# Moving the last quarter of a set-up weight product into the first graph's chain of products

## The chip, the cores and the metric

One core of one Trainium2 chip runs the whole program. The metric is the device time of one execution, in microseconds (us).

## The reference, cut to what matters

There are 64 graphs of 256 nodes and 512 features. Each passes a graph layer with a residual and a norm, then an attention layer with the same frame:

```python
def L0(x, adj, W):                                 # layer 0
    deg = jnp.sum(adj, axis=-1, keepdims=True)
    agg = jnp.einsum('bij,bjf->bif', adj, x) / jnp.maximum(deg, EPS)
    return jax.nn.relu(jnp.einsum('bnf,of->bno', jnp.concatenate([x, agg], axis=2), W))
def L1(X, adj, mask, Wqk, Wv):                     # layer 1
    q, k = jnp.split(X @ Wqk, 2, axis=-1)
    v = X @ Wv
    agg = jnp.einsum('bij,bjd->bid', adj, k * mask[:, :, None])
    w = inv_scale * mask * jnp.einsum('bid,bid->bi', q, agg)
    return jax.nn.softmax(w, axis=1)[:, :, None] * v
x = _layernorm(x + L0(x, adj, L0_gnn_W))
x = _layernorm(x + L1(x, adj, nodemask, L1_gnn_Wqk, L1_gnn_Wv))
```

The kernel never forms q and k. It multiplies the two halves of `Wqk` once, at the start. This "product of weights" is a 512x512x512 float32 product, and its result `w1[:, :4]` is used by layer 1 alone. Layer 1 of the first graph begins at about 66 to 69 us, long after its layer 0.

## The kernel before

The set-up product: 16 matmul instructions, which the profile shows as 32 records (two for each float32 instruction), all ahead of the first graph.

```python
ps = [ps_mm.tile([P, F], F32, name="mm") for _ in range(NF)]
for a in range(NA):                                # NA = NF = 4
    for c in range(NF):
        nc.tensor.matmul(ps[c], wqk[:, a, c * P:(c + 1) * P], wqk[:, NA + a, :], start=(a == 0), stop=(a == NA - 1))
for c in range(NF):
    nc.scalar.copy(w1[:, c, :], ps[c])
```

Every other product is done by a scheme with seven products instead of eight. It needs sums of the weights (on VectorE, once for each layer) and of the rows (for each graph, on GpSimd for layer 0 and on VectorE for layer 1). The four sums of a layer are called T1 to T4 here:

```python
def weight_sums(w, name):                          # W0 for layer 0, W1 for layer 1
    ...
    nc.vector.tensor_sub(t1, b12, b11)             # T1
    nc.vector.tensor_sub(t2, b22, t1)              # T2
    nc.vector.tensor_sub(b12, b22, b12)            # T3
    nc.vector.tensor_sub(t4, b21, t2)              # T4
```

Layer 0 of a graph is five products, then two. The sixth waits until `u` has been copied out, and the gather with `adj` waits for the last addition. The first graph has nothing else to run in these two waits. Later graphs run layer 1 of an earlier graph there.

```python
def layer0_a(g):
    ...                                            # u = A11.B11; p5 = S1.T1; u += S2.T2; p2 = A12.B21
    product(u, s["S3"], w["T3"], start=False)
    nc.scalar.copy(y[:, 1, :], u)                  # the sixth product waits for this
    nc.vector.tensor_add(y[:, 1, :], p5, y[:, 1, :])
def layer0_b(g):
    product(u, s["A22"], w["T4"], start=False)     # sixth
    nc.scalar.copy(own[:, 1, :], u)
    product(p5, s["S4"], w["B22"], start=False)    # seventh
    nc.vector.tensor_add(y[:, 0, :], p5, y[:, 0, :])   # the gather waits for this
```

The gather makes four sums `tv` on VectorE, seven half-width products on TensorE and additions into `zr`. The norm's chain follows: `combine0` and `layer_norm` on VectorE, masked copies on ScalarE, then a transpose.

The loop over graphs, cut:

```python
W0 = weight_sums(w0, "t0_")
for i in range(B + LAG - 1):
    if i == 1:
        W1 = weight_sums(w1, "t1_")
    ...
    layer0_a(i)
    ...
    layer0_b(i)
    ...                                            # gather, combine0, norm0
```

The order of instructions on an engine is not the order of these lines: a scheduler sets it. `tc.issue_after(x)` holds the instructions of its block behind `x` in that order.

Of the kernel before, what the change touches and what calls it, by code (L numbers as in the profile page):

```python
# [35 lines left out]
F32 = mybir.dt.float32  # L36
# [4 lines left out]
P = 128  # L41
Q = 32
LAG = 4
DEG_EPS = 1e-6
LN_EPS = 1e-5
# [3 lines left out]
def resnorm_kernel(  # L49
# [12 lines left out]
    nc = tc.nc  # L62
    B, N, F = x.shape
    A = wqk_t.shape[0] // 2
    NT, NF, NA = N // P, F // P, A // P
    H, HF = NF // 2, F // 2
# [4 lines left out]
    const = ctx.enter_context(tc.tile_pool(name="const", bufs=1))  # L71
    pool = ctx.enter_context(tc.tile_pool(name="pool", bufs=2))
    small = ctx.enter_context(tc.tile_pool(name="small", bufs=4))
    ps_mm = ctx.enter_context(tc.tile_pool(name="ps_mm", bufs=8, space=bass.MemoryType.PSUM))
# [5 lines left out]
    def first(out, in_):  # L80

        return tc.keep_in_program_order(nc.sync.dma_start(out, in_))

    def load(g, dma=nc.sync.dma_start):
        adjs[g] = pool.tile([P, NT, N], F32, name="adj", bufs=4)
        dma(adjs[g], adj_t[g].rearrange("(t p) i -> p t i", p=P))
        rows[g] = pool.tile([P, NT, N], F32, name="rows")
        dma(rows[g], adj[g].rearrange("(t p) j -> p t j", p=P))
        xs[g] = pool.tile([P, NT, F], F32, name="x", bufs=3)
        dma(xs[g], x[g].rearrange("(t p) f -> p t f", p=P))  # L90
        return load_t(g, dma)

    def load_t(g, dma):
        if g not in xTs:
            xTs[g] = pool.tile([P, NF, N], F32, name="xT")
            return dma(xTs[g], x_t[g].rearrange("(c p) n -> p c n", p=P))


    w0 = const.tile([P, 2 * NF, F], F32, name="w0")
    w1 = const.tile([P, 2 * NF, F], F32, name="w1")  # L100
    setup = tc.tile_pool(name="setup", bufs=1)
    with setup as sp:
        wqk = sp.tile([P, 2 * NA, F], F32, name="wqk")
        for a in range(NA):
            src = wqk_t.rearrange("(h a p) f -> a p h f", p=P, h=2)[a]
            first(wqk.rearrange("p (h a) f -> a p h f", h=2)[a], src)
        w0_of = w_t.rearrange("(k h p) o -> k p h o", p=P, h=H)
        for k in (0, 2):
            first(w0[:, k * H:(k + 1) * H, :], w0_of[k])
        load_t(0, first)  # L110
        for k in (3, 1):
            first(w0[:, k * H:(k + 1) * H, :], w0_of[k])
        load(0, first)
        mask_sb = const.tile([P, NT, B], F32, name="mask_sb")
        first(mask_sb, mask_t)
        load_t(1, first)
        load(1, first)
        loaded = first(w1[:, NF:, :], wv.rearrange("(c p) o -> p c o", p=P))

        ident = const.tile([P, P], F32, name="ident")  # L120
        make_identity(nc, ident)
        eps = const.tile([P, 1], F32, name="eps")
        nc.vector.memset(eps, LN_EPS)
        wide = [const.tile([P, Q], F32, name=f"wide{k}") for k in (0, 1)]
        for w in wide:
            nc.vector.memset(w, 0.0)

        ps = [ps_mm.tile([P, F], F32, name="mm") for _ in range(NF)]
        for a in range(NA):
            for c in range(NF):  # L130
                nc.tensor.matmul(ps[c], wqk[:, a, c * P:(c + 1) * P], wqk[:, NA + a, :],  # L131
                                 start=(a == 0), stop=(a == NA - 1))
        for c in range(NF):
            nc.scalar.copy(w1[:, c, :], ps[c])
    late = ctx.enter_context(tc.tile_pool(name="late", bufs=2))

    def weight_sums(w, name):
        b11, b21, b12, b22 = (w[:, k * H:(k + 1) * H, :] for k in range(4))
        t1, t2, t4 = (const.tile([P, H, F], F32, name=f"{name}{k}") for k in (1, 2, 4))
        nc.vector.tensor_sub(t1, b12, b11)  # L140
        nc.vector.tensor_sub(t2, b22, t1)  # L141
        nc.vector.tensor_sub(b12, b22, b12)
        nc.vector.tensor_sub(t4, b21, t2)
        return {"B11": b11, "B21": b21, "B22": b22, "T1": t1, "T2": t2, "T3": b12, "T4": t4}
# [13 lines left out]
    def product(ps, a, b, start=True):  # L158
        for c in range(H):
            nc.tensor.matmul(ps, a[:, c, :], b[:, c, :], start=start and c == 0, stop=(c == H - 1),  # L160
                             skip_group_check=True)

    def bank():
        return ps_mm.tile([P, F], F32, name="mm")
# [26 lines left out]
    def prepare(g):  # L191
        deg = small.tile([P, NT], F32, name="deg")
        r = rows.pop(g)
        for t in range(NT):
            nc.scalar.activation(r[:, t, :], r[:, t, :], AF.Copy, accum_out=deg[:, t:t + 1])
        rdegs[g] = small.tile([P, NT], F32, name="rdeg")
        nc.vector.tensor_scalar(rdegs[g], deg, DEG_EPS, None, op0=OP.max)
        nc.vector.reciprocal(rdegs[g], rdegs[g])
        a, sa = adjs[g], pool.tile([P, 4, P], F32, name="sa", bufs=3)
        a11, a21, a12, a22 = a[:, 0, :P], a[:, 0, P:], a[:, 1, :P], a[:, 1, P:]  # L200
        nc.gpsimd.tensor_add(sa[:, 0], a21, a22)  # L201
        nc.gpsimd.tensor_sub(sa[:, 1], sa[:, 0], a11)
        nc.gpsimd.tensor_sub(sa[:, 2], a11, a21)
        nc.gpsimd.tensor_sub(sa[:, 3], a12, sa[:, 1])
        sumsA[g] = {"A11": a11, "A12": a12, "A22": a22, "S1": sa[:, 0], "S2": sa[:, 1], "S3": sa[:, 2],
                    "S4": sa[:, 3]}
        sums0[g] = row_sums(xTs.pop(g), nc.gpsimd)

    def layer0_a(g):
        s, w = sums0[g], W0  # L210
        own = owns[g] = pool.tile([P, NT, F], F32, name="own")
        y = values(g)[:, 0]
        u, p5, p2 = bank(), bank(), bank()
        product(u, s["A11"], w["B11"])
        began = nc.scalar.copy(own[:, 0, :], u)  # L215
        product(p5, s["S1"], w["T1"])
        product(u, s["S2"], w["T2"], start=False)
        nc.scalar.copy(y[:, 0, :], u)
        product(p2, s["A12"], w["B21"])
        added = nc.vector.tensor_add(own[:, 0, :], p2, own[:, 0, :])  # L220
        product(u, s["S3"], w["T3"], start=False)
        nc.scalar.copy(y[:, 1, :], u)  # L222
        nc.vector.tensor_add(y[:, 1, :], p5, y[:, 1, :])
        open0[g] = u, p5
        return began, added

    def layer0_b(g):
        s, w, own, y = sums0.pop(g), W0, owns[g], values(g)[:, 0]
        u, p5 = open0.pop(g)
        product(u, s["A22"], w["T4"], start=False)  # L230
        nc.scalar.copy(own[:, 1, :], u)
        product(p5, s["S4"], w["B22"], start=False)
        nc.vector.tensor_add(y[:, 0, :], p5, y[:, 0, :])  # L233

    def values(g):

        if g not in vals:
            vals[g] = pool.tile([P, 2, NT, F], F32, name="vals")
        return vals[g]
# [68 lines left out]
    def layer1_steps(g):  # L308
        sc, part = scores[g] = (small.tile([P, NT], F32, name="scores", bufs=3),
                                small.tile([P, 1], F32, name="part", bufs=3))  # L310
        s, w, agg = sums1.pop(g), W1, aggs.pop(g + 1)[:, 1]
        v = vs[g] = late.tile([P, NT, F], F32, name="v", bufs=LAG)
# [87 lines left out]

    W0 = weight_sums(w0, "t0_")
    prepare(0)
    def step(gen, n=1):
        for _ in range(n):
            next(gen, None)

    for i in range(B + LAG - 1):
        new = i < B
        if i + 2 < B:
            with tc.issue_after(loaded.ins):  # L410
                loaded = load(i + 2)
        if i == 1:
            W1 = weight_sums(w1, "t1_")
        if 0 <= i - 3 < B - 2:
            write_scores(i - 3)
            read_scores(i - 3)
        if new:
            began, added = layer0_a(i)
        if 0 <= i - 2 < B:
            turn(i - 2)  # L420
        l1 = layer1_steps(i - 2) if 0 <= i - 2 < B else iter(())
        step(l1)
        if new:
            layer0_b(i)
        if i - 3 >= B - 2:
            softmax_turned(i - 3)
            finish(i - 3)
        if i <= B:
            z, summed = gather_a(i)
        step(l1, 2)  # L430
        step(z)
        if 0 <= i - LAG < B - 2:
            with tc.issue_after(began.ins), tc.issue_after(added.ins):
                softmax(i - LAG)
            with tc.issue_after(summed.ins):
                finish(i - LAG)
        for _ in range(4):
            step(l1)
            step(z)
        if new:  # L440
            combine0(i)
            norm0(i)
        if i + 1 < B:
            with tc.issue_after(began.ins), tc.issue_after(added.ins):
                prepare(i + 1)
# [26 lines left out]
```

## Time and profile before

| kernel before | |
|---|---|
| time, median of 3 runs | 1988.32 us (1986.9 to 1988.72) |
| profiled span | 1986.5 us |
| set-up product: first matmul to the first layer-0 product | 15.60 us (4.67 to 20.27) |
| first layer-0 product (A) to first product of the fourth graph (M) | 70.64 us (20.27 to 90.91): **S** |
| M to the first layer-1 product of the last graph but one | 1848.0 us (90.91 to 1938.92) |
| from there to the end | 47.6 us |

The row marked S begins after TensorE's wait for the first load and after its warm-up, and it ends when TensorE has been without a gap for some 20 us. The prediction shows TensorE's side of the start. This is VectorE's timeline of the same stretch (start in us, length, engine, line, operation, output<-inputs, shape, count, and in brackets the idle time before with its releaser):

```profile
29.68 0.69 DVE L223 TENSOR_TENSOR vals<-mm,vals 128x512 f32<-128x512 f32 x1 [1.03 <-ACT vals L222]
30.28 1.22 DVE L140 TENSOR_TENSOR t<-w 128x1024 f32<-128x1024 f32 x1
...
32.68 1.22 DVE L142 TENSOR_TENSOR w<-w 128x1024 f32<-128x1024 f32 x1
33.81 0.68 DVE L233 TENSOR_TENSOR vals<-mm,vals 128x512 f32<-128x512 f32 x1
...
41.53 0.75 DVE L291 SCALAR_TENSOR_TENSOR own<-zr,rdeg,own 128x512 f32<-128x512 f32 x1 [0.81 <-ACT zr L281]
...
46.05 0.66 DVE L220 TENSOR_TENSOR own<-mm,own 128x512 f32<-128x512 f32 x1
46.74 1.00 DVE L188 TENSOR_SCALAR x<-own,mv,rstd 128x512 f32<-128x512 f32 x2
```

Three of layer 1's sums (from 30.28 us) stand ahead of the addition of line 233, for which the gather waits. The chain of the first norm begins at 41.53 and has its result `x` from 46.74 on, 5.21 us later.

### The profile page before, as it was taken

Reading aid. Unit: us, or ns where it says so; the run is one execution under the profiler, and the core shown is the slowest. Engines: PE = TensorE matmul, PEld = TensorE weight load, DVE = VectorE, ACT = ScalarE, POOL = GpSimd, SP = SyncE. Lnnn points to the kernel's source line nnn. Section 1 sums busy time; section 2 is a strip of 40 time slices with the busy share of each in tenths; the row PEclk is TensorE's granted clock in tenths of the full one; section 3 lists DMA queues with packets and bytes.
Section 4 is the critical chain, followed back from the end, with each engine's and each line's share of the span. In section 5 each row is a group of like instructions: output and inputs, shape, how many; then the busy total and the mean of one; then the engine's idle time right before and its main releaser. Section 6 shows DMA issues by size and latency. Waiting matters only on the chain.

```text
span 1986.5 us, 19676 instructions
## 1 busy us (share of the span) xinstructions
PE 1960.3 (99%) x5416; PEld 1017.5 (51%) x5416; DVE 1566.5 (79%) x3218; ACT 650.0 (33%) x1543; POOL 419.6 (21%) x518
## 2 busy tenths in 40 slices
PE   8999999999999999999999999999999999999996
PEld 3554555555555545555555555555555555555552
DVE  5677877888788788778878887887787788878877
ACT  2323333333233333333332333333333333323332
POOL 3122221221221221222212212212222122122100
PEclk9999999999999999999999999999999999999999
DMA  6333333333333333333333333333333333333221
GB/s 223 88 83 82 98 94 85 95 91 90 96 80 100 93 83 103 93 81 95 91 90 95 83 98 94 83 102 93 81 95 92 89 96 81 101 96 80 80 45 56
DMA packets 394830, 182.62 MB, mean 92 GB/s; under 512 B 285793, under 2 KB 359393, under 8 KB 394721
## 3 DMA queue, kind: packets, MB, share of 16 engines
q1 hardware_dynamic: 394720, 181.36, 34.0%
q8 instruction: 44, 0.72, 0.2%
q14 instruction: 66, 0.53, 0.1%
HBM read 114.10 MB, written 33.62 MB: 74 GB/s over the span
## 4 chain that ended last, share of the span: by engine, by line
PE 96%; DVE 1%; SPq 1%; DMA 0%; ACT 0%; issue 0%; DVEq 0%
PE mm L160 76%; PE mm L259 19%; SPq L175 1%; PE mm L131 1%; DVE st L182 0%; DMA adj<-adj_t 0%; DMA wqk<-wqk_t 0%; DVE own L293 0%; DVE own L291 0%; DMA x1T<-sq 0%; DVE x L188 0%; DVE o L396 0%; ACT vals L300 0%; DVE v L341 0%; DVE t L141 0%
## 5 line engine op out<-in xcount | busy, mean ns | idle before, releaser
L160 PE MATMUL mm<-w,s 128*128 128x512 f32 x1024 | 481.5, 592 | 0.8 <-ACT v L327 0.8
L160 PE MATMUL mm<-t,s 128*128 128x512 f32 x1024 | 461.4, 593 | 0.2 <-ACT q L320 0.2
L160 PEld LDWEIGHTS mm<-t,s 128*128 128x128 f32 x1024 | 194.7, 190 | 243.7 <-issue 228.2
L160 PEld LDWEIGHTS mm<-w,s 128*128 128x128 f32 x1024 | 194.2, 190 | 192.8 <-issue 155.0
L160 PE MATMUL mm<-w,x1T 128*128 128x512 f32 x512 | 241.4, 594 | 3.9 <-DMA x1T<-sq 3.9
L160 PE MATMUL mm<-w,xT 128*128 128x512 f32 x512 | 240.9, 592 | 0.0
L201 POOL TENSOR_TENSOR sa<-adj 128x128 f32<-128x128 f32 x64 | 45.8, 716 | 760.2 <-PE mm L259 758.7
L152 POOL TENSOR_TENSOR s<-xT 128x256 f32<-128x256 f32 x64 | 46.8, 731 | 706.3 <-PE mm L160 687.3
L259 PE MATMUL mm<-tv,sa 128*128 128x256 f32 x768 | 187.4, 379 | 0.6 <-DVE tv L249 0.4
L259 PEld LDWEIGHTS mm<-tv,sa 128*128 128x128 f32 x768 | 145.7, 190 | 76.3 <-issue 48.2
L233 DVE TENSOR_TENSOR vals<-mm,vals 128x512 f32<-128x512 f32 x64 | 44.2, 691 | 142.9 <-PE mm L160 142.9
L185 ACT ACTIVATE rstd<-mv,eps 128x2 f32<-128x2 f32 x128 | 37.9, 296 | 341.3 <-DVE mv L183 341.3
L160 PEld LDWEIGHTS mm<-w,x1T 128*128 128x128 f32 x512 | 97.2, 190 | 98.9 <-issue 95.6
L160 PEld LDWEIGHTS mm<-w,xT 128*128 128x128 f32 x512 | 97.3, 190 | 94.7 <-issue 91.4
L327 ACT COPY v<-mm 128x512 f32<-128x512 f32 x64 | 37.5, 586 | 284.8 <-PE mm L160 284.8
L160 PE MATMUL mm<-t,xT 128*128 128x512 f32 x256 | 126.8, 617 | 2.8 <-ACT vals L222 2.8
L160 PE MATMUL mm<-t,x1T 128*128 128x512 f32 x256 | 125.4, 612 | 0.9 <-ACT v L334 0.9
L291 DVE SCALAR_TENSOR_TENSOR own<-zr,rdeg,own 128x512 f32<-128x512 f32 x128 | 107.6, 841 | 22.0 <-ACT zr L281 21.9
L259 PE MATMUL mm<-vals,adj 128*128 128x256 f32 x512 | 121.3, 379 | 1.9 <-DVE vals L233 1.9
L259 PEld LDWEIGHTS mm<-vals,adj 128*128 128x128 f32 x512 | 97.1, 190 | 43.6 <-issue 16.7
L215 ACT COPY own<-mm 128x512 f32<-128x512 f32 x64 | 37.5, 586 | 227.4 <-PE mm L160 227.4
L316 DVE SCALAR_TENSOR_TENSOR q<-mm,zr 128x512 f32<-128x512 f32 x128 | 86.1, 673 | 32.4 <-PE mm L160 32.4
(89 smaller groups left out, 2729.5 us busy)
## 6 DMA issues: line engine op xcount, KB each, us to landing
xT<-x_t SPq DMA_DIRECT2D x64, 512.0 KB
x<-x SPq DMA_DIRECT2D x64, 512.0 KB
x1T<-sq SPq DMA_DIRECT2D x1024, 32.0 KB
out<-o SPq DMA_DIRECT2D x64, 512.0 KB
adj<-adj_t SPq DMA_DIRECT2D x64, 256.0 KB
rows<-adj SPq DMA_DIRECT2D x64, 256.0 KB
row<-d SPq DMA_DIRECT2D x62, 128.0 KB
d<-turned SPq DMA_DIRECT2D x248, 0.2 KB
```

Of the source, the lines that this page charges most:

```text
L131: nc.tensor.matmul(ps[c], wqk[:, a, c * P:(c + 1) * P], wqk[:, NA + a, :], start=(a == 0), stop=(a == NA - 1))
L152: eng.tensor_add(s1, a21, a22)
L160: nc.tensor.matmul(ps, a[:, c, :], b[:, c, :], start=start and c == 0, stop=(c == H - 1), skip_group_check=True)
L175: nc.sync.dma_start(to[b * Q:(b + 1) * Q, :, a, :], sq[a * Q:(a + 1) * Q, b].rearrange("p c t q -> p (c t) q"))
L185: nc.scalar.activation(rstd, mv[:, :, 1], AF.Ln, bias=eps)
L201: nc.gpsimd.tensor_add(sa[:, 0], a21, a22)
L215: began = nc.scalar.copy(own[:, 0, :], u)
L233: nc.vector.tensor_add(y[:, 0, :], p5, y[:, 0, :])
L259: nc.tensor.matmul(ps[:, k * HF:(k + 1) * HF], sumsA[g - k][a], w[b][:, n, :], start=start and n == 0, stop=True, skip_group_check=True)
L291: nc.vector.scalar_tensor_tensor(own[:, t, :], z[:, t, :], rdeg[:, t:t + 1], own[:, t, :], op0=OP.mult, op1=OP.add)
L316: nc.vector.scalar_tensor_tensor(q, a, 1.0, agg[:, t, :], op0=OP.mult, op1=OP.mult, accum_out=to)
L327: nc.scalar.copy(v[:, 0, :], u)
```

## The change

**Intent:** TensorE idles twice in the first graph's chain, 0.68 and 1.15 us by the profile. Three quarters of the product of weights stay ahead of the first graph; the last quarter is cut in two halves of two matmul instructions, and each half is put into one of the two waits. The pool of `wqk` is closed later, and the sums for layer 1 come into a new order on VectorE.

```diff
-        ps = [ps_mm.tile([P, F], F32, name="mm") for _ in range(NF)]
-        for a in range(NA):
-            for c in range(NF):
-                nc.tensor.matmul(ps[c], wqk[:, a, c * P:(c + 1) * P], wqk[:, NA + a, :],
-                                 start=(a == 0), stop=(a == NA - 1))
-        for c in range(NF):
-            nc.scalar.copy(w1[:, c, :], ps[c])
-    late = ctx.enter_context(tc.tile_pool(name="late", bufs=2))
+    def weight_product(chunks, pause=NA):
+        ps = [ps_mm.tile([P, F], F32, name="mm") for _ in chunks]
+        for a in range(NA):
+            for k, c in enumerate(chunks):
+                nc.tensor.matmul(ps[k], wqk[:, a, c * P:(c + 1) * P], wqk[:, NA + a, :],
+                                 start=(a == 0), stop=(a == NA - 1))
+            if a + 1 == pause:
+                yield
+        for k, c in enumerate(chunks):
+            nc.scalar.copy(w1[:, c, :], ps[k])
+        yield
+    def step(gen, n=1):
+        for _ in range(n):
+            next(gen, None)
+    step(weight_product((0, 1, 2)), 2)
 ... (loads: same, only indented otherwise) ...
+    rest = weight_product((3,), NA // 2)
     for i in range(B + LAG - 1):
         if i == 1:
+            setup.close()
+            late = ctx.enter_context(tc.tile_pool(name="late", bufs=2))
             W1 = weight_sums(w1, "t1_")
         if new:
             began, added = layer0_a(i)
+        if i == 0:
+            step(rest)
 ...
         if new:
             layer0_b(i)
+        if i == 0:
+            step(rest)
```

More of the change, by code (lines that the diff above doesn't have):

```diff
@@ L100, in resnorm_kernel @@
     w1 = const.tile([P, 2 * NF, F], F32, name="w1")
-    setup = tc.tile_pool(name="setup", bufs=1)
-    with setup as sp:
-        wqk = sp.tile([P, 2 * NA, F], F32, name="wqk")
-        for a in range(NA):
-            src = wqk_t.rearrange("(h a p) f -> a p h f", p=P, h=2)[a]
-            first(wqk.rearrange("p (h a) f -> a p h f", h=2)[a], src)
-        w0_of = w_t.rearrange("(k h p) o -> k p h o", p=P, h=H)
-        for k in (0, 2):
-            first(w0[:, k * H:(k + 1) * H, :], w0_of[k])
-        load_t(0, first)
-        for k in (3, 1):
-            first(w0[:, k * H:(k + 1) * H, :], w0_of[k])
-        load(0, first)
-        mask_sb = const.tile([P, NT, B], F32, name="mask_sb")
-        first(mask_sb, mask_t)
-        load_t(1, first)
-        load(1, first)
-        loaded = first(w1[:, NF:, :], wv.rearrange("(c p) o -> p c o", p=P))
-        ident = const.tile([P, P], F32, name="ident")
-        make_identity(nc, ident)
-        eps = const.tile([P, 1], F32, name="eps")
-        nc.vector.memset(eps, LN_EPS)
-        wide = [const.tile([P, Q], F32, name=f"wide{k}") for k in (0, 1)]
-        for w in wide:
-            nc.vector.memset(w, 0.0)
-        ps = [ps_mm.tile([P, F], F32, name="mm") for _ in range(NF)]
-        for a in range(NA):
-            for c in range(NF):
-                nc.tensor.matmul(ps[c], wqk[:, a, c * P:(c + 1) * P], wqk[:, NA + a, :],
-                                 start=(a == 0), stop=(a == NA - 1))
-        for c in range(NF):
-            nc.scalar.copy(w1[:, c, :], ps[c])
@@ L135, in resnorm_kernel @@
-    late = ctx.enter_context(tc.tile_pool(name="late", bufs=2))
+    setup = ExitStack()
+    wqk = setup.enter_context(tc.tile_pool(name="setup", bufs=1)).tile([P, 2 * NA, F], F32, name="wqk")
+    for a in range(NA):
+        src = wqk_t.rearrange("(h a p) f -> a p h f", p=P, h=2)[a]
+        first(wqk.rearrange("p (h a) f -> a p h f", h=2)[a], src)
+    w0_of = w_t.rearrange("(k h p) o -> k p h o", p=P, h=H)
+    for k in (0, 2):
+        first(w0[:, k * H:(k + 1) * H, :], w0_of[k])
+    load_t(0, first)
@@ new lines, in resnorm_kernel @@
+    for k in (3, 1):
+        first(w0[:, k * H:(k + 1) * H, :], w0_of[k])
+    load(0, first)
+    mask_sb = const.tile([P, NT, B], F32, name="mask_sb")
+    first(mask_sb, mask_t)
+    load_t(1, first)
+    load(1, first)
+    loaded = first(w1[:, NF:, :], wv.rearrange("(c p) o -> p c o", p=P))
+    ident = const.tile([P, P], F32, name="ident")
+    make_identity(nc, ident)
+    eps = const.tile([P, 1], F32, name="eps")
+    nc.vector.memset(eps, LN_EPS)
+    wide = [const.tile([P, Q], F32, name=f"wide{k}") for k in (0, 1)]
@@ new lines, in resnorm_kernel @@
+    for w in wide:
+        nc.vector.memset(w, 0.0)
+    def weight_product(chunks, pause=NA):
+        ps = [ps_mm.tile([P, F], F32, name="mm") for _ in chunks]
+        for a in range(NA):
+            for k, c in enumerate(chunks):
+                nc.tensor.matmul(ps[k], wqk[:, a, c * P:(c + 1) * P], wqk[:, NA + a, :],
+                                 start=(a == 0), stop=(a == NA - 1))
+            if a + 1 == pause:
[3 more added lines that the diff above has]
+        yield
@@ L402, in resnorm_kernel @@
     prepare(0)
-    def step(gen, n=1):
-        for _ in range(n):
-            next(gen, None)
+    rest = weight_product((3,), NA // 2)
     for i in range(B + LAG - 1):
```

## The prediction

> **What bounds the kernel now.** I read the page's busy shares first, then the table of engines by stretch (cut at 75 and 1940 us), then TensorE's timeline of the first 110 us with the VectorE and ScalarE timelines beside it, and last how the two programs order their instructions on each engine.
>
> The busy shares name TensorE:
>
> ```profile
> PE 1960.3 (99%) x5416; PEld 1017.5 (51%) x5416; DVE 1566.5 (79%) x3218; ACT 650.0 (33%) x1543; POOL 419.6 (21%) x518
> ```
>
> The stretches (from:to, length, TensorE busy, then the other engines, granted clock, DMA share, GB/s) say where the idle time is:
>
> ```profile
> 75.00:1940.00 1865.00, 1865.00 (x5179) 973.50 (x5178) 1492.45 (x3064) 618.39 (x1464) 399.31 (x484) 1.00 0.34 89
> 0.00:75.00 75.00, 64.92 (x164) 31.01 (x165) 41.09 (x72) 21.43 (x50) 20.31 (x35) 1.00 0.56 178
> 1940.00:1987.00 47.00, 30.39 (x76) 12.97 (x74) 32.95 (x84) 10.23 (x29) 0.00 (x0) 0.90 0.20 59
> ```
>
> From 75 to 1940 us TensorE has no idle time. All of it lies at the start (10.1 us) and the end (16.6 us). The change adds and removes no matmul and touches only the start, so its reach is those 10.1 us, of which 4.67 are the wait for the first load. What is left, 5.4 us, stands in TensorE's timeline (start, length, group, and in brackets the idle time before it with its releaser):
>
> ```profile
> 4.67 15.76 PE L131 MATMUL mm<-wqk 128*128 128x512 f32 x32 [4.67 <-DMA wqk<-wqk_t]
> 20.27 1.88 PE L160 MATMUL mm<-w,xT 128*128 128x512 f32 x4
> ...
> 27.14 1.88 PE L160 MATMUL mm<-w,s 128*128 128x512 f32 x4
> 29.70 1.98 PE L160 MATMUL mm<-t,xT 128*128 128x512 f32 x4 [0.68 <-ACT vals L222]
> 31.52 1.88 PE L160 MATMUL mm<-w,s 128*128 128x512 f32 x4
> 34.55 1.13 PE L259 MATMUL mm<-vals,adj 128*128 128x256 f32 x4 [1.15 <-DVE vals L233]
> 36.11 0.67 PE L259 MATMUL mm<-tv,sa 128*128 128x256 f32 x2 [0.43 <-DVE tv L249]
> ...
> 37.84 0.67 PE L259 MATMUL mm<-tv,sa 128*128 128x256 f32 x2 [0.20 <-DVE tv L250]
> ...
> 49.17 1.98 PE L160 MATMUL mm<-t,xT 128*128 128x512 f32 x4 [1.65 <-ACT vals L222]
> 50.99 1.88 PE L160 MATMUL mm<-w,s 128*128 128x512 f32 x4
> 53.66 1.99 PE L259 MATMUL mm<-vals,adj 128*128 128x256 f32 x8 [0.78 <-DVE vals L233]
> ```
>
> The idle figure counts from the modelled end of the last matmul. I count from where the next could have begun: full-speed groups of four 512-column records follow each other 1.714 us apart (25.42 to 27.14), so a record takes 0.4285 us, and one of 256 columns half of that. By this measure the first graph's gaps are 29.70 - 28.85 = 0.85 us, plus 0.10 because the group after it took 1.82 instead of 1.71; 34.55 - 33.24 = 1.31; 36.11 - 35.41 = 0.70; 37.84 - 37.40 = 0.44; and 49.17 - 47.37 = 1.80. Each of the first two has a product of the same graph waiting for an accumulator to be copied out or added, and nothing else for TensorE to do.
>
> **What the Trainium skill says.** "TensorE: Matmul & The Clock Gate", section "What's actually happening", says the cold start is a budget of time (about 3.4 us), not a number of matmuls. The trace agrees: the first records of the weight product stand 0.86 us apart until 8.25 us, 3.6 us after the start, and 0.43 us apart after that. So what is taken out of the product at 4.67 us is worth full-speed records. "SBUF — State Buffer", the section on the access model with the table of doors, says that a VectorE operation with two SBUF inputs and a GpSimd operation reading SBUF exclude each other for a whole instruction. The trace agrees in kind: the subtraction for tv of 128x256 took 0.41 us at 35.55, and 0.94 us at 35.88 and at 36.75, while GpSimd's sums ran. "Trace analysis" in the skill ("Perfetto Trace Analysis", section "Identifying the Most-Contended Engine") warns that matmul busy time is no measure of distance to the roofline; here I use it only to find idle time, which it can show.
>
> **The change, part by part.**
>
> Removed at the front: a quarter of the 32 records, 8 x 0.4285 = 3.43 us. The first graph's first product can then start at 20.27 - 3.43 = 16.84. Its inputs must be there: the VectorE sums of its weights stand at 11.5 to 19.2 us and GpSimd's sums of xT at 12.97 to 16.7. The product that uses the last of them (t of line 143, ready at 19.20) comes at 27 us, so none is late. The slices of wqk are needed after 6 records each instead of 8; the DMA moves 388 GB/s in this stretch, so 0.52 MB lands each 1.4 us after 4.64, and the second is wanted only at about 8.7. No wait there.
>
> Put back: two halves of two matmuls, 4 x 0.4285 = 1.71 us each. The order of the changed program's TensorE instructions shows them just ahead of the two products that wait now. Chain: five products from 16.84 end at 25.41. The first half runs to 27.13. The ScalarE copy that released the old wait needs 0.16 + 0.59 us, so it is done by 26.2: the 0.95 us gap is gone. Two products to 30.56, the second half to 32.27. VectorE's addition (0.69 us) can be done at 31.45, if VectorE is free. In the kernel before it was not: the three sums of the second layer's weights, 1.22 us each, stood ahead of it. In the new order only one of them does, 27.8 to 29.0. So the gap of 1.31 is gone too.
>
> Then the sums on VectorE. One (1.22 us) stands between the addition and the first tv, 31.4 to 32.65, so tv is ready at about 33.05 and TensorE asks for it at 32.27 + 0.86 = 33.13: the gap of 0.70 falls to about 0.05. The other two sums, 2 x 1.22 = 2.44 us, which in the kernel before ran ahead of tv, now stand after the last tv and ahead of the addition to zr (line 278 before) which the last product of the gather must await, since it accumulates in the same bank. VectorE: three more tv and one zr (1.9 to 2.9 us, by how GpSimd collides) to 35.2 to 35.8, the two sums to 37.7 to 38.4, the zr addition to 38.1 to 38.8. TensorE would want that bank at 37.5 to 37.9. **A new gap of about 0.6 us** appears there.
>
> It is partly paid already. The 1.80 us gap at 49.17 comes from ScalarE, which does the masked copies of the first norm before the copy that TensorE wants; and these hang on VectorE's combine and norm, 41.53 to 47.7 us, begun right after the gather's last ScalarE copy at 41.5. In the new program that chain begins when VectorE is through with the zr addition, 38.1 to 38.8, which is 2.7 to 3.4 us earlier. The products of the second graph arrive up to 2.2 to 2.8 us earlier, and that gap shrinks by the difference. After it all work is shifted by what the VectorE chain has gained; the later gaps (0.78 and 0.51 us) are distances between TensorE's own results and their consumers, and move along.
>
> Sum: 0.95 + 1.31 + 0.65 = 2.9 us gained by TensorE up to 35 us, a new gap of about 0.6 against it, as much regained at 49 us: **2.9 us**, about 0.15%. The steady part, at 30.3 us for each graph with no idle time, passes the shift to the end unchanged. 1988.3 - 2.9 = 1985.4; the profiled run took 1988.24 for a span of 1986.5, so the span should be 1983.6.
>
> **The rivals.** First, the halves are hidden nowhere: the start is bound by loads, and the product only filled a wait for them; the time stays 1988.3. For it: the DMA queues are at 370 to 388 GB/s up to 20 us. Against: no gap of TensorE between 4.67 and 29.06 us, and all operands of the first products had landed by 17.7.
>
> Second, VectorE becomes the bound: the two displaced sums collide with GpSimd (1.80 and 1.74 us instead of 1.22 when they did at 14 to 18 us) and delay the zr addition and with it the norm's chain by over 1 us. Then the gain is some 1.5 to 2 us, 1986.5. For it: GpSimd's sums of the third graph start when its xT lands, now about 33 us, just ahead of them. Against: at 0.4 to 0.9 us each, GpSimd is nearly done when the sums start.
>
> Third, everything hides, the collision with tv falls away as GpSimd starts later in VectorE's order, and the 0.44 us gap goes too: 3.4 us, 1984.9.
>
> A second-order effect is that a shift of the whole program meets another phase of the clock gate at the end, where the mean clock is 0.90 and some matmuls run slow: an estimate of 0.5 us either way, from the four records of 2.6 us there that would take 1.9 at full speed.
>
> **Range and chances.** The runs of before spread over 1.8 us (1986.9 to 1988.72), as much as half the effect. 1985.4 with about 1.6 us each way: 1983.8 to 1987.2. For 2% the time would have to move by 40 us, and the change touches 10 us of idle time: within 2% is as good as certain. A slower kernel needs a change in the repeated part, and the order of instructions of all five engines is the same from the second graph on.
>
> **What would show it.** Right: L131's successor has 24 records at the front, ending 3.4 us earlier, and two groups of 4 with no idle time before or after; no wait for vals at the first graph; a wait of 0.3 to 0.9 us before the gather's last product for VectorE's zr; the first saturated stretch (70.95 before) starting at 68.0; span 1983.6. Wrong: a DMA wait before the first product, a wait for vals still at the first graph, or the shift at 100 us not found at the end. The claim fails as a whole if the mean time falls by less than 1 us or more than 4.5.

## The result, and the profile after

| | before | after |
|---|---|---|
| time, median (runs) | 1988.52 us (6, 1986.9 to 1990.27) | 1985.7 us (6, 1985.16 to 1986.67) |
| ratio | | 0.9986, 95% interval 0.9973 to 0.9999 |
| profiled span | 1986.5 us | 1983.4 us |
| first matmul to A | 15.60 us | 12.52 us |
| S (A to M) | 70.64 us | 71.15 us |

A ratio is always the mean time of one kernel's fast runs over that of the other's of the same rounds, so not quite the ratio of the medians in the table. The time fell by 2.8 us, 0.14%: within 2%, at the predicted place (1985.4). The interval only just leaves out 1.

TensorE by stretch (from:to, length, then busy time of TensorE, weight loads, VectorE, ScalarE, GpSimd, clock, DMA share, GB/s), after:

```profile
0.00:75.00 75.00, 67.19 (x170) 32.57 (x171) 43.35 (x75) 21.32 (x50) 25.64 (x37) 1.00 0.56 180
```

TensorE is busy for 2.27 us more in the first 75 us (64.92 before), with six more records of work. The steady stretch is at 1865.00 of 1865.00 us as before. TensorE's timeline after:

```profile
4.58 12.68 PE L132 MATMUL mm<-wqk 128*128 128x512 f32 x24 [4.58 <-DMA wqk<-wqk_t]
17.10 1.88 PE L169 MATMUL mm<-w,xT 128*128 128x512 f32 x4
...
25.68 1.88 PE L132 MATMUL mm<-wqk 128*128 128x512 f32 x4
...
30.83 1.88 PE L132 MATMUL mm<-wqk 128*128 128x512 f32 x4
...
38.46 0.70 PE L268 MATMUL mm<-vals,sa 128*128 128x256 f32 x2 [0.58 <-DVE zr L287]
...
46.52 1.98 PE L169 MATMUL mm<-t,xT 128*128 128x512 f32 x4 [1.36 <-ACT vals L231]
...
68.30 1.98 PE L169 MATMUL mm<-t,xT 128*128 128x512 f32 x4 [0.51 <-ACT vals L231]
```

Both halves (25.68 and 30.83) stand without idle time before or behind them, and both `vals` waits of the first graph are gone. The wait at 38.46 is new: the gather's last product stands for VectorE's addition to `zr` (line 287). The wait of the second graph (46.52) has shrunk from 1.65 to 1.36. M is reached at 88.25:

```profile
88.25 1.88 PE L169 MATMUL mm<-w,xT 128*128 128x512 f32 x4
```

and before:

```profile
90.91 1.88 PE L160 MATMUL mm<-w,xT 128*128 128x512 f32 x4
```

That is a shift of 2.66 us. VectorE after shows where the new wait comes from:

```profile
31.03 0.69 DVE L242 TENSOR_TENSOR vals<-mm,vals 128x512 f32<-128x512 f32 x1 [2.13 <-PE mm L169]
...
34.65 1.75 DVE L151 TENSOR_TENSOR w<-w 128x1024 f32<-128x1024 f32 x1
36.32 1.75 DVE L152 TENSOR_TENSOR t<-w,t 128x1024 f32<-128x1024 f32 x1
37.99 0.41 DVE L287 TENSOR_TENSOR zr<-mm,zr 128x256 f32<-128x256 f32 x1
38.51 0.75 DVE L300 SCALAR_TENSOR_TENSOR own<-zr,rdeg,own 128x512 f32<-128x512 f32 x1
...
43.48 0.69 DVE L229 TENSOR_TENSOR own<-mm,own 128x512 f32<-128x512 f32 x1 [0.34 <-PE mm L169]
44.09 0.99 DVE L197 TENSOR_SCALAR x<-own,mv,rstd 128x512 f32<-128x512 f32 x2
```

T3 and T4 of layer 1 (lines 151, 152) now stand between the last `tv` and the `zr` addition. They took 1.75 us each, where the same sums took 1.22 before. GpSimd's row sums of the third graph ran at the same time:

```profile
35.27 1.71 POOL L162 TENSOR_TENSOR s<-s,xT 128x256 f32<-128x256 f32 x1
37.06 1.59 POOL L164 TENSOR_TENSOR s<-xT,s 128x256 f32<-128x256 f32 x1
```

At the end of VectorE's excerpt, the norm's scaling (line 197) stands behind the second graph's addition of line 229, and that one waited 0.34 us for a product of the second graph. So from the chain's start to its `x` it took 5.58 us (38.51 to 44.09) against 5.21 before.

### The profile page after: what moved, and what is told of

Its sections match the earlier page's. It is cut to its first block, busy times and chain, and to the rows that moved or that the text cites. A ratio compares the mean times of both kernels' runs of the same rounds, so it can differ in the third digit from the quotient of the medians.

```text
span 1983.4 us, 19675 instructions
## 1 busy us (share of the span) xinstructions
PE 1959.9 (99%) x5416; PEld 1017.8 (51%) x5416; DVE 1566.6 (79%) x3218; ACT 649.8 (33%) x1543; POOL 421.3 (21%) x518
## 4 chain that ended last, share of the span: by engine, by line
PE 97%; DVE 1%; ACT 0%; DMA 0%; SPq 0%; issue 0%; DVEq 0%
PE mm L169 77%; PE mm L268 19%; PE mm L132 1%; SPq L184 0%; DMA wqk<-wqk_t 0%; DVE st L191 0%; DMA rows<-adj 0%; ACT vals L309 0%; DVE own L302 0%; DMA x1T<-sq 0%; DVE t L152 0%; DVE w L151 0%; DVE own L300 0%; DVE o L405 0%; DVE vals L242 0%
```

## The experiments

**Theory.** The move pays because each half fills its own wait. What it doesn't pay is due to VectorE's order: T3 and T4 stand ahead of the `zr` addition, and the norm's scaling behind the second graph's addition. **Rival 1:** the filling is worth little; the gain comes from the changed order of VectorE, since the sums of layer 1 no longer stand in the second wait. **Rival 2:** it doesn't matter in which wait the matmuls stand.

| kernel | first matmul to A | A | M | S | span |
|---|---|---|---|---|---|
| before | 15.60 | 20.27 | 90.91 | 70.64 | 1986.5 |
| after | 12.52 | 17.10 | 88.25 | 71.15 | 1983.4 |
| after, again | 11.88 | 16.20 | 87.36 | 71.16 | 1980.3 |
| after, late sums | 12.27 | 16.68 | 86.48 | 69.80 | 1983.0 |
| before, late sums | 15.27 | 19.74 | 88.09 | 68.35 | 1982.4 |
| late sums, no quarter | 12.64 | 17.04 | 85.64 | 68.60 | 1980.3 |
| late sums, all in the first wait | 12.15 | 16.57 | 87.42 | 70.85 | 1980.4 |
| late sums, all in the second wait | 13.28 | 17.70 | 88.44 | 70.74 | 1983.1 |
| late sums, parts of 1, 1, 2 | 12.39 | 16.77 | 85.89 | 69.12 | 1980.2 |
| late sums, 1, 1, 2 and 1 more | 11.73 | 16.11 | 85.23 | 69.12 | 1980.2 |
| sums ahead again | 12.78 | 17.16 | 88.03 | 70.87 | 1981.8 |
| norm first | 12.85 | 17.38 | 88.20 | 70.82 | 1984.3 |

S came out the same to 0.01 us in the two traces of the changed kernel. "First matmul to A" did not, nor did the span; more on that in the next section.

### The changed kernel with the sums later

The halves stay where they are. T1 and T2 of layer 1 are made as soon as their weights are there, and T3 and T4 behind the second graph's additions.

```diff
+        if i == 0:
+            second, others, W1 = weight_sums(w1, "t1_")   # T1, T2
+        if i == 1:
+            with tc.issue_after(summed_y.ins):             # behind the second graph's addition to y
+                others()                                   # T3, T4
-            W1 = weight_sums(w1, "t1_")
```

Cut from this diff: T2 is held ahead of the first graph's last addition, and each half behind the product that it follows in the changed kernel too.

> The changed kernel with the last two sums of the second layer's weights moved behind the second graph's first addition, so that they no longer stand ahead of the addition to zr, and the first two pinned ahead of the first graph's last addition. Measure: S, the time from the start of the first layer-0 product to the start of the fourth graph's first product, which leaves out the warm-up; it is 70.64 us in the kernel before and 71.15 in the changed one. Theory (the halves fill two waits of the first graph, the displaced sums give 0.6 us back): the 0.58 us idle ahead of the gather's last product goes, the second graph's wait grows back to about 1.7, S is 70.5, time some 0.6 us under the changed kernel. Rival (the order of the sums is off the path): S stays 71.1.

Measured: S 69.80, 1.35 us less than the changed kernel, and more than expected. Time 1985.24 us median of 4 (1983.43 to 1985.76), ratio to before 0.999 (0.9973 to 1.0007). TensorE and then VectorE of this kernel:

```profile
36.44 0.59 PE L273 MATMUL mm<-vals,sa 128*128 128x256 f32 x2
...
44.75 1.98 PE L171 MATMUL mm<-t,xT 128*128 128x512 f32 x4 [0.85 <-ACT vals L234]
```

```profile
37.10 0.75 DVE L305 SCALAR_TENSOR_TENSOR own<-zr,rdeg,own 128x512 f32<-128x512 f32 x1 [0.92 <-ACT zr L295]
```

The new wait of the gather is gone (no bracket at 36.44), the norm's chain starts 20.42 us after A instead of 21.41, and the second graph's wait is at 0.85. But this kernel does not isolate the place of the sums. The scheduler had also moved one matmul instruction of the second graph (two records, 0.86 us) behind the first graph's gather, and the norm's scaling ahead of the addition that waits. The last two experiments separate these.

### The kernel before with the sums later

The same edit to the kernel before: all 16 matmuls ahead of A, the sums out of the way.

> The kernel before, whole product at the front, with the same moved sums. Theory: the first wait (0.85 + 0.10 us) stays, the second falls from 1.31 to 0.9 because the addition no longer stands behind a sum, the gaps of 0.70 and 0.44 at tv go; S falls from 70.64 to about 69.1, time 1.5 us under before. Rival (the gain of the change is only a better order of VectorE's work, the halves hide nothing): S falls to about 67.7, i.e. the whole 2.9 us without moving a matmul. Rival (the order of the sums is off the path): S stays 70.6.

Measured: S 68.35 and time 1985.11 us (1984.21 to 1985.31), ratio 0.999 (0.9975 to 1.0005). With the sums out of the way in both, filling makes S longer by 69.80 - 68.35 = 1.45 us and the front shorter by 3.43 (8 records at 0.4285). So **the filling alone is worth 1.98 us**; rival 1 falls. The order has a part, though: it was costing the kernel before 70.64 - 68.35 = 2.29 us and the changed kernel 71.15 - 69.80 = 1.35, and the 0.94 between them is the rest of the change's gain. The whole times do not show this: in the same rounds the two kernels had 1985.24 and 1985.11 us. In their traces the late-sums change is 1.6 us ahead at M, and its end is 2.2 us longer (see "The end of the program" below).

### No quarter at all

The moved matmuls are left out, to weigh them where they stand. The result is wrong (relative error 0.039).

```diff
-    rest = weight_product((3,), NA // 2)
+    rest = iter(())
+        nc.scalar.copy(w1[:, 3, :], ps[2])      # any finite values
```

> Wrong result on purpose: as e1_late_sums, but the last quarter of the product is not computed at all; its place in the weights gets a copy of another quarter. Theory: S as in e2_before_late_sums, 69.1, as the waits are open again; e1 minus this one is the price of the 3.43 us of moved matmuls where they now stand: 1.4 us, so 2.0 of 3.43 us are hidden. Rival (the halves are fully hidden): S is 70.5 as in e1. Rival (the halves hide nothing): S is 67.1.

Measured: S 68.60, time 1982.06 us (1981.64 to 1982.11), ratio 0.9975 (0.996 to 0.999). The moved matmuls cost 69.80 - 68.60 = 1.20 us where they stand, so 2.23 of their 3.43 us are hidden. The two waits are there again in this kernel:

```profile
26.46 1.98 PE L172 MATMUL mm<-t,xT 128*128 128x512 f32 x4 [0.68 <-ACT vals L235]
...
31.18 1.13 PE L274 MATMUL mm<-vals,adj 128*128 128x256 f32 x4 [1.02 <-DVE vals L247]
```

Each half is 1.71 us long, and the waits, counted from where the next matmul could have begun, are 0.84 and 1.19 (26.46 - 23.91 - 1.714 and 31.18 - 28.28 - 1.714). With 0.10 of slower restart behind each, that makes the 2.23. The comparison with "before, late sums" gave 1.98, as its second wait was 0.24 shorter (33.65 - 30.98 - 1.714 = 0.96): here VectorE's T2, 1.36 us long beside GpSimd's sums, stands right ahead of the addition. In both, what is hidden is the size of the waits. A half that is longer than its wait pushes the chain by the rest.

### One, one and two

So the halves are cut to fit: one matmul in each of these two waits, and two in the second graph's wait, which had 0.85 us idle left.

```diff
-    rest = weight_product((3,), NA // 2)
+    rest = weight_product((3,), (1, 2, NA))     # pauses after the first and the second
+        if i == 1:
+            with tc.issue_after(last.ins):       # behind layer0_a of the second graph
+                step(rest, 2)
```

> As e1_late_sums, but the quarter's four matmuls stand as one, one and two: one each in the two waits of the first graph, two in the second graph's wait ahead of the same product. Theory: each wait of 0.95, 0.9 and 1.8 us takes its matmuls (0.86, 0.86, 1.71) nearly whole, S is 69.1 to 69.4, and with the front 3.43 us shorter the time is 4.5 to 5 us under before. Rival (what counts is only that the quarter leaves the front): S is 70.5 as in e1.

```profile
25.36 1.02 PE L132 MATMUL mm<-wqk 128*128 128x512 f32 x2
...
42.54 1.88 PE L132 MATMUL mm<-wqk 128*128 128x512 f32 x4
```

Measured: S 69.12, time 1982.02 us (1981.9 to 1983.62), ratio 0.9977 (0.9962 to 0.9992). No idle time stands at any of the three. Only 69.12 - 68.60 = 0.52 of the 3.43 us is paid now, and S is as expected. The third wait was not the 1.8 us of the expectation, though: without the quarter it is 43.91 - 41.18 - 1.714 = 1.02 in the trace, so the two matmuls there (1.71) are about 0.6 too long for it.

### All four in the first wait, and all four in the second

```diff
-                step(rest, 1)                    # one half behind layer0_a, one behind layer0_b
+                step(rest, 2)                    # both behind layer0_a (or both behind layer0_b)
```

> As e1_late_sums, but all four matmuls of the quarter stand in the first of the two waits, none in the second. S is 69.80 us in e1 and 68.60 without the quarter. Theory (each half hides only in its own wait): 3.43 us stand in a wait of 0.95, and the second wait of 0.96 opens again: S is 70.8, 1.0 us over e1. Rival (only the removal from the front matters, the place behind it doesn't): S is 69.8.

> As e1_late_sums, but all four matmuls stand in the second wait. Theory: the first wait of 0.95 us for the copy of vals opens again, the second, 1.19 us without the quarter, is filled: S is 70.8, as in e4_all_first. Rival (place doesn't matter): 69.8.

Measured: S 70.85 and 70.74; times (2 runs each) 1983.33 and 1985.89 us, ratios 0.998 (0.9962 to 0.9999) and 0.9993 (0.9975 to 1.0012). S is about 1 us above the 69.80 of the split in halves, since the other wait opens again. With all in the first, the second:

```profile
32.97 1.13 PE L273 MATMUL mm<-vals,adj 128*128 128x256 f32 x4 [0.79 <-DVE vals L246]
```

With all in the second, the first:

```profile
27.12 1.98 PE L171 MATMUL mm<-t,xT 128*128 128x512 f32 x4 [0.68 <-ACT vals L234]
```

Rival 2 falls: a matmul hides only in the wait it stands in.

### A fifth matmul

One more instruction, the last of the third quarter, goes behind the seventh product of the second graph, where `vals` is waited for again. T4 moves behind the second graph's `tv` sums.

```diff
+        if i == 1:
+            with tc.issue_after(last.ins):       # behind layer0_b of the second graph
+                remainder()                      # fifth matmul and its copy
```

> As e6_1_1_2, with a fifth matmul, the last of the third quarter, taken from the front and placed in the second graph's second wait (0.96 us ahead of its gather); the last sum of the weights moves behind the second graph's tv. Theory (a wait takes a matmul of 0.86 us whole): S stays 69.1, the front is 0.86 us shorter, time some 0.8 us under e6 and 5 under before. Rival (something else, like VectorE's addition, comes late by as much): S grows to 70.0 and the time is that of e6.

Measured: S 69.12, with a front of 22 records instead of 24, so the fifth is free. Time 1981.68 us (5 runs, 1980.81 to 1981.98), ratio 0.997 (0.9957 to 0.9984). It is correct and the best version found. In the same rounds the changed kernel had 1983.49, and the means are 1981.5 and 1983.5.

### The changed kernel once more

> The changed kernel itself once more, for its difference to before on the same chip as the others. Theory: 2 to 3.5 us under before in the medians, with S of 71.15 us within 0.1; what else differs between executions is the warm-up of TensorE (up to 0.8 us) and the end of the program (46.3 to 48.5 us from the last saturated stretch on in the traces so far).

Measured: S 71.16, time 1983.49 us (5 runs, 1982.09 to 1985.66), ratio 0.9981 (0.9969 to 0.9994). S repeats; the front does not (11.88 against 12.52 us). The whole time misses its expectation: the median is 4.3 us under before (1987.78 in these rounds), not 2 to 3.5. Other expected whole times were missed as well: "before, late sums" came out 1.0 us under before (1.5 expected), 1, 1, 2 came out 4.1 under (4.5 to 5), and the fifth matmul 6.1 under (5).

### The sums ahead again, with the late-sums order on TensorE

T3 and T4 go back to where the changed kernel has them; TensorE keeps the late-sums order, apart from the gather's last product, which stands behind one matmul more of the second graph.

```diff
-            with tc.issue_after(summed_y.ins):
-                others()
+        if i == 0:
+            with tc.issue_after(summed.ins):     # behind the last tv
+                second = others()                # and the zr addition behind them
```

> S is the time from the start of the first layer-0 product to the start of the fourth graph's first product (changed kernel 71.15 and 71.16 us in two runs; the changed kernel with late sums 69.80). That kernel with late sums differed from the changed one by more than the place of the two sums of the second half: one product of the second graph had also moved behind the first graph's gather (0.86 us), and the norm's scaling of the first graph had moved ahead of the second graph's addition to its own rows (0.37 us). This kernel keeps the TensorE order of the late-sums kernel but puts the two sums back between the last gather copy and the addition that ends the first graph's rows. If the sums lie on the path there: S 70.4 when each takes about 1.22 us and part is hidden by the addition's other wait, 70.7 if they collide with GpSimd's instructions at 1.75 us each. Rival, the place of the sums is worth nothing and the moved product was worth all: S 69.8 as with late sums. Span of the slowest core 0.6 to 0.9 us above the late-sums kernel at equal warm-up, or nothing.

```profile
34.53 1.74 DVE L153 TENSOR_TENSOR w<-w 128x1024 f32<-128x1024 f32 x1
36.20 1.75 DVE L154 TENSOR_TENSOR t<-w,t 128x1024 f32<-128x1024 f32 x1
...
38.38 0.75 DVE L306 SCALAR_TENSOR_TENSOR own<-zr,rdeg,own 128x512 f32<-128x512 f32 x1
```

```profile
38.33 0.70 PE L273 MATMUL mm<-vals,sa 128*128 128x256 f32 x2 [0.40 <-DVE zr L293]
```

Measured: S 70.87, time 1984.15 us (1983.6 to 1986.27), ratio 0.9977 (0.996 to 0.9993). The place of the two sums costs 70.87 - 69.80 = **1.07 us**, more than either figure expected. The one matmul that stands ahead of the gather's last product again is not what sets the time there: TensorE was through with it and waited 0.40 us for the `zr` addition, which stood behind T4. The norm's chain starts 21.22 us after A instead of 20.42, which is 0.80. The rest is in the chain itself: 5.47 us to its `x` instead of 5.21, because the last `zr` addition came later (39.77 here) and stands behind both steps of the first half of the rows. So the rival (the moved matmul did it all) falls, by the trace and not by the edit alone.

### The norm first

The changed kernel with the second graph's addition held behind the norm's scaling on VectorE; TensorE's order is unchanged.

```diff
+        with tc.issue_after(normed.ins) if g == 1 else ExitStack():
             added = nc.vector.tensor_add(own[:, 0, :], p2, own[:, 0, :])
```

> The changed kernel with one order alone changed: on VectorE the second graph's addition to its own rows, which in the trace of the changed kernel stood 0.34 us idle for TensorE, comes behind the first graph's norm scaling instead of ahead of it. TensorE's order is the changed kernel's. Theory: this is the 0.37 us that the first graph's chain lost after its addition, so S (first layer-0 product to the fourth graph's first product) goes from 71.15 to about 70.8, and the chain from the addition to the norm's result takes 5.2 us rather than 5.58. Rival: the second graph's wait absorbs it, S stays 71.15 plus or minus 0.05.

```profile
44.02 1.00 DVE L197 TENSOR_SCALAR x<-own,mv,rstd 128x512 f32<-128x512 f32 x2 [0.60 <-ACT rstd L195]
```

Measured: S 70.82, time 1985.1 us (1983.14 to 1987.13), ratio 0.9978 (0.9963 to 0.9993). From the chain's start (38.79) to `x` it took 5.23 us, and S is 0.33 below the changed kernel's 71.15, as the theory said. So the 1.35 us of the late-sums kernel fall into 1.07 for the place of the sums and 0.28 between the changed kernel (71.15) and the sums-ahead kernel (70.87). The latter has the norm's scaling ahead, which is worth 0.33 by itself, and two of the gather's products one matmul earlier, for which nothing is left.

## Why the prediction was right

The predicted time (1985.4, range 1983.8 to 1987.2) held, and the measured 1985.7 lies in the range. Step by step:

**The front.** Predicted 3.43 us off, with A at 16.84. Measured 3.08 and 17.10. The records removed are the predicted eight; the rest is warm-up. The weight load at which the pace changes from 0.85 to 0.43 us is the first of these before, and the second after:

```profile
8.25 0.20 PEld L131 LDWEIGHTS mm<-wqk 128*128 128x128 f32 x1 [0.52 <-issue]
```

```profile
8.95 0.19 PEld L132 LDWEIGHTS mm<-wqk 128*128 128x128 f32 x1 [0.45 <-issue]
```

The cost of warming up is the front's length less its records at 0.4285: 15.60 - 32 x 0.4285 = 1.89 before and 12.52 - 24 x 0.4285 = 2.24 after. The difference is the missing 0.35. Nothing speaks for its being the change's doing: the same changed kernel had 11.88 - 10.28 = 1.60 in its second trace. The prediction took the warm-up as the same in both.

**No wait for data.** Right: the 24 records of the front are one group, and only the first load is waited for. One reading was off without harm: the last weight sum of layer 0 (T4, ready at 19.20) is used by the sixth product, at 29.70 us before, and not at 27.

**The two waits.** Right: both halves fill them, predicted 0.95 and 1.31 us.

**The tv gaps.** Predicted: 0.70 falls to 0.05, and 0.44 stays. Measured: both are gone. GpSimd's sums began at 33.60 us, when three of VectorE's four `tv` sums, 0.42 us each, were all but done, so they hardly collided with them. That was the third rival's mechanism.

**The new gap.** Predicted about 0.6; measured 38.46 - 37.28 - 0.43 = 0.75, and 0.10 for a slow restart. The step said that the sums would take 1.22 us each, since GpSimd would be nearly done. They took 1.75 each, as the second rival said. So the mechanisms of the second and the third rival both came true in part and worked against each other: 0.44 + 0.05 gained, 0.25 lost here.

**The regain.** Predicted: the second graph's gap (1.80) gives back about 0.6, as all is shifted in the end by what VectorE's chain gains. Measured: the gap is 46.52 - 43.28 - 1.71 = 1.53, so it gave back 0.27: the second graph's products came 2.37 us earlier (47.37 to 45.00 by the same count), the norm's result only 2.65 (46.74 to 44.09). The step "shifted by what the VectorE chain has gained" was not exact. The chain's start gained 41.53 - 38.51 = 3.02, but the shift at M was 2.66: the chain itself became 0.37 us longer because of the order that the norm-first kernel undoes.

**The sum.** Gaps counted from the next possible start: 0.95 + 1.31 + 0.70 + 0.44 - 0.85 = 2.55 up to the second graph, with some 0.1 of slow restarts more, and 0.27 there. At equal warm-up this is 3.43 - (71.15 - 70.64) = **2.92 us**, predicted 2.9. So the sum was right while its terms were off in opposite directions (0.49 us more at `tv`, 0.25 less at the new gap, 0.33 less at the second graph). That they cancel to 0.02 us is luck.

**To the end.** Predicted an unchanged steady part and span 1983.6. Measured 1848.0 us for the part behind M in both, and a span of 1983.4. Warm-up took 0.35 from the gain, and the tail gave 0.4 back: from the first layer-1 product of the last graph but one to the end it took 47.2 us instead of 47.6. That the two cancel is luck as well: the second rounds of the changed kernel gave a difference of 4.3 us in the medians.

**The end of the program.** The whole times rank the late-sums kernel (S 69.80) no better than the changed kernel. In these traces warm-up costs 1.56 to 3.00 us and the tail lasts 45 to 48.5, which is more than most differences in S. The traces show which part of the tail varies. TensorE waits once more there, for the transposed rows of the last graph (tile `x1T`, by DMA). In all twelve traces the tail takes 16.2 us to the start of the last matmul group ahead of this wait (0.6 us long), and 19.0 to 19.2 us from the next product of `w` and `x1T` behind it to the end. In between lie the wait, 2.66 to 3.87 us, and a stretch from the product that waited to that next one, 6.58 to 8.96 us, in which matmuls often go slowly: the first group of four takes 1.95 to 3.75 us. These are the first groups behind the wait in the first and the second trace of the same changed kernel, whose tails are 47.2 and 45.0 us:

```profile
1956.47 2.37 PE L169 MATMUL mm<-w,x1T 128*128 128x512 f32 x4 [3.46 <-DMA x1T<-sq]
```

```profile
1954.68 1.95 PE L169 MATMUL mm<-w,x1T 128*128 128x512 f32 x4 [2.68 <-DMA x1T<-sq]
```

The late-sums kernel had the long kind of both (3.79 and 8.94 us), and "before, late sums" had 2.67 and 7.85: this is the 2.2 us that covers its lead at M. The prediction counted the slow matmuls as a second-order effect of 0.5 us; they alone differ by up to 2.4 us between traces.

**What stays open.** What sets the length of this DMA wait and of the slow stretch is not shown, and each kernel's tail is known from one trace only, except the changed kernel's. The fifth-matmul kernel stands in the same rounds 2.0 us below the changed kernel in the mean, where S and the front at equal warm-up give 71.16 - 69.12 + 0.86 = 2.9.

## What to carry to other kernels

Work moved from the front into waits is hidden only up to the length of the wait it stands in, so cut the pieces to the waits: two halves of 1.71 us in waits of about 1 us hid 2.0 to 2.2 of 3.43 us, while 1, 1 and 2 hid 2.91. When a move changes the order on a second engine, look there for what it puts ahead of the next addition that TensorE needs: here two sums that no product needed for another 40 us cost 1.07 us. Where effects are smaller than the spread of whole runs, measure a distance within the trace that leaves warm-up and end out, and run one kernel twice to see how well it repeats.

## What the Trainium skill lacked or had wrong

- "TensorE: Matmul & The Clock Gate", section "What's actually happening", puts the warm-up at about 3.4 us and its end at ±500 ns. As a cold record takes twice the time here (0.85 against 0.43 us), the cold stretch is twice the costs above: 3.1 us (before, late sums), 3.2 (the changed kernel's second trace), 3.8 (before), 4.5 (the changed kernel's first trace) and 6.0 (all in the second wait, where the slow pace lasted from 4.42 to 10.40 us). The spread is far wider than ±0.5 us. The same section does warn that the number of cold matmuls varies from run to run, which fits the traces better than its ±500 ns; for a comparison of a few us it should give the spread as a time.
- "SBUF — State Buffer", section "SBUF: two separate sides", says that of two colliding instructions one fully blocks. What it lacks is the size over a run of them: two sums of 1.22 us took 3.42 together (34.65 to 38.07) beside GpSimd's sums, and GpSimd's took 1.71 and 1.59 where they take 0.72 or 0.73 alone. Both engines lost, and the loss lay on the path.
